# A feed-forward's first bias moved into its weights, relu and split in one ScalarE pass, the inverse root on GpSimd

## The chip, the core and the metric

The kernel runs on one core of a Trainium2 chip. The time is that of the device from the first to the last instruction of the program, in microseconds; the lower the better. Of three runs before the change the median is 1888.09 us (1886.04 to 1891.85). The profile is of one further execution.

The engines, as the profile names them: PE (TensorE's matrix multiplications) and PEld (its weight loads), DVE (VectorE), ACT (ScalarE), POOL (GpSimd), and SP (SyncE, which here only issues transfers). Each engine works through its own queue in order.

## What is computed

A macaron block on x of shape (8, 2048, 256), all in float32: half a feed-forward, a state space layer (SSM) with a skip and a layer norm, half a feed-forward.

```python
def _layernorm(x, axis=-1, eps=1e-05):
    m = jnp.mean(x, axis=axis, keepdims=True)
    v = jnp.var(x, axis=axis, keepdims=True)
    return (x - m) / jnp.sqrt(v + eps)

# feed-forward; w1 is (256, 1024), w2 is (1024, 256)
    h = jax.nn.relu(jnp.einsum('bsd,dw->bsw', x, w1) + b1)
    return jnp.einsum('bsw,wd->bsd', h, w2) + b2

# SSM: K is a kernel of 2048 lags per channel, from the parameters
    z = y + x * D[None, None, :]          # y = causal convolution of x with K
    r = x + z
    out = (r - mu) * jax.lax.rsqrt(var + LN_EPS) * ln_w + ln_b

# the block
    x = x + 0.5 * _L0_ffn_ref(_layernorm(x, axis=-1), ...)
    x = x + _L0_attn_ref(_layernorm(x, axis=-1), ...)
    x = x + 0.5 * _L0_ffn_ref(_layernorm(x, axis=-1), ...)
```

Both feed-forwards have the same weights. Their layer norm has no weights of its own, so the 256 normalised channels of a token sum to zero.

## The kernel before

**Tiling.** The 16384 tokens are worked in 64 groups of 256 (two tiles of 128 tokens, `NTB = 2`). A feed-forward goes through the groups one by one (`sublayer`, L807). Each group has 8 steps, one for each block of 128 hidden units. A step multiplies up (`up`, L782: 6 matmuls of 128x128 by 256 columns), applies relu, and three steps later (`LAG = 3`) multiplies that block down (`down`, L793: 6 matmuls). So a group has 96 matmuls of 256 columns.

**Float32 out of three products.** Every factor is split into a rounded high part (type float32r) and a low part. A product is high x low + low x high + high x high, hence three matmuls for each. Weights are split once (`load_weights`, L149), the group's input once a group (xh, xl), and each hidden block once a step (hh, hl). The hidden block's path is: PE writes `ph` in PSUM; ScalarE applies relu with the first bias in place (L857); ScalarE copies the high part to `hh` (L858); VectorE subtracts to get the low part `hl` (L859). Four PSUM banks hold `ph`.

**The group's input.** `ffn_in` (L709) takes the group's rows, makes mean and variance on VectorE (`stats`, L659), the half root on ScalarE (`root`, L670), a polished inverse root on VectorE (`rstds`, L676: four instructions on 128x2 numbers), and normalises (`norm`, L686). In groups 0 to 11 of the first feed-forward (`ACT_NORM = 12`) the normalisation runs on ScalarE, elsewhere on VectorE. GpSimd then adds half the second bias to the rows (L719). The normalised rows are turned by PE in groups 0 to 13 and 19 to 43 of the first feed-forward and 0 and 1 of the second (L726, then xh on ScalarE L735 and xl on VectorE L737). In the others they are turned by the DMA engines in two 16-bit halves (`turn_by_dma`, L742: halves apart on both engines L747, store, transposing load, halves together L765, xh L767, xl L769). The buffer `xn` of the normalised rows is single and is shared with `y` of the second feed-forward and with `sw` of the convolution.

**The order of work.** `pre_a` and `pre_b` (L893, L1118) make a group's input in steps, one for each step of the loop, and begin 18 and 19 steps ahead of the group's turn. `post_a` (L903) adds the group's output, stores x1, and normalises it into `u`, the SSM's input, with another root and polish; `post_b` (L1144) adds and stores. During the first feed-forward a background generator (`matrices`, L234, then `early`, L1050) makes the SSM's matrices from the parameters: first some 150 small steps on VectorE, then tables on GpSimd, then for 32 batches six products of 128x512 on GpSimd (`make`, L557, lines L570 to L580). Each batch is then split, stored, and transposed by DMA (L590, L620). The background is handed out by a budget: each loop step adds 1.32, and a batch of matrices takes 8.0 of it. Apart from that the order on each engine is that of a planner, which simulates the program and puts instructions in queues as they become ready; before the first group ScalarE and VectorE keep program order.

**The second feed-forward.** `pre_b` loads x1 through SP's queue into `xb`, has GpSimd add the layer norm's bias (L1125), makes statistics of the convolution's output on VectorE, root and polish, `y` (L1135) and then x2 (L1138), and goes through `ffn_in`. `xb` has five buffers.

Of the kernel before, what the change touches and what calls it, by code (L numbers as in the profile page):

```python
# [29 lines left out]
# pi / 2 in four parts, the first three of eight bits each  # L30
# [13 lines left out]
def macaron_s4d_kernel(  # L44
# [25 lines left out]
    NJ = L // P           # chunks of 128 positions  # L70
    CB = (NJ - 1) * B     # columns (chunk, batch) of the chunks that have a next one
    NQ = 4                # quarters of the sequence
# [3 lines left out]
    NTB = 2               # token tiles in a group  # L76
    TOK = NTB * P
    NG = NJ * B // NTB    # groups
    GPJ = B // NTB        # groups in a chunk
# [3 lines left out]
    NZ = 1  # L83
    PINF = 0
# [3 lines left out]
    NU = NFC // 2         # units of two blocks of the hidden layer  # L88
    SLOTS = 2 * NU        # steps in a group

    NPAIR = H // 2        # channels h = 2 g + c; (c, n) on the partitions
    NK = 8                # powers w**(2**k)
    NA, NB = 8, 16        # w**(16 a + b), below 128
    BCH = 8               # channels in a batch of matrices, in two parts
    NBT = H // BCH
    HCH = BCH // 2
    PB = BCH // 2         # pairs in a batch
    KROW = 256            # the lags from 128 to 0, then 127 zeros
# [9 lines left out]
    BUFS = {"e": 1, "te": 1, "x": 5, "xn": 1, "xh": 2, "xl": 2, "hh": 4, "hl": 4, "pl": 2, "g": 1, "gt": 1}  # L108
# [4 lines left out]
    def slot(tag, shape, name, dtype=F32):  # L113
        tag = {"sw": "xn"}.get(tag, tag)
        return work.tile(shape, dtype, name=name, tag=tag, bufs=BUFS[tag])

# [9 lines left out]
    # The SSM's input, then its output in place: [position in chunk, chunk, batch, channel].  # L126
    u = upool.tile([P, NJ, B, H], F32, name="u")
    # Until their quarters of the input come: room for the SSM's matrices.
# [4 lines left out]
    # ------------------------------------------------------------- weights  # L133
# [6 lines left out]
    b1_sb = const.tile([P, NFC], F32, name="b1_sb")  # L140
    hb2 = const.tile([P, H], F32, name="hb2")
    eps4 = const.tile([P, 1], F32, name="eps4")
    V.memset(eps4, 0.25 * EPS)
    A_.activation(stat.tile([P, 1], F32, name="warm", tag="s"), eps4, AF.Sqrt)
# [4 lines left out]
    def load_weights():  # L149
# [4 lines left out]
        raw2 = room[1][:, NDC * W : NDC * W + NFC * H].rearrange("p (f m) -> p f m", m=H)  # L154
        w2v = w2.rearrange("(fc p) m -> p fc m", p=P)
        for i in range(4):
# [3 lines left out]
            )  # L160
        for i in range(2):
            fs = slice(4 * i, 4 * i + 4)
            W2Q[i].dma_start(out=raw2[:, fs], in_=w2v[:, fs, :])
        for _ in range(7):
            yield
        for i in range(4):
            fs = slice(i * q, (i + 1) * q)
            hi = w1t[0][:, :, fs]
            A_.copy(hi, raw1[:, i])
# [18 lines left out]
    # ------------------------------------------------------- the SSM's matrices  # L188
    # P[n, k] = p0 w**k with p0**2 = 2 Ct w: a chunk's state is sum_k P[n, 127 - k] u[k], and
    # position i of the next chunk takes Re(sum_n P[n, i] state[n]).  # L190
# [4 lines left out]
    # w**128, and its imaginary part with the signs for the conjugate states  # L195
# [27 lines left out]
    def vsqrt(o, v, t, s, pace):  # L223
        """o = sqrt(v), to float32's precision."""
# [481 lines left out]
    def halves(xt):  # L706
        return [xt[:, i, :] for i in range(NTB)]
# [481 lines left out]
```

## Time and profile before

| | us |
|---|---|
| median of three runs | 1888.09 |
| the profiled execution, its span | 1885.0 |
| first matmul of the first feed-forward | 9.2 |
| first feed-forward, up to its last relu | 857.4 |
| second feed-forward, first to last relu | 1139.8 to 1877.5 |
| PE busy | 1813.4 (96%) |
| DVE busy | 1566.6 (83%) |
| ACT busy | 1267.4 (67%) |
| POOL busy | 726.0 (39%) |

How to read the rows. In the page's slices each digit is the busy share of one fortieth of the span in tenths. PEclk is the clock that TensorE was granted, in tenths of full speed. A row of groups reads: line, engine, operation, output<-inputs, shape, count | busy us, mean ns of one | idle time of the engine just before, and what ended it. A row of waits reads: who waited <- for whom: total us, times, longest us. A row of the chain or of the timeline: start us, length us, what. A busy PE is not PE at its full rate, since matmuls overlap; the distance from start to start tells that.

### The profile page before, as it was taken

To read this page: it belongs to the slowest core of one execution; us is meant where nothing else is said; L and a number is where in the kernel's file an instruction comes from. 1 tells how busy PE (TensorE), PEld (TensorE's weight loads), DVE (VectorE), ACT (ScalarE), POOL (GpSimd) and SP (SyncE) were. 2 spreads that over 40 slices of the span, in tenths; PEclk is the share of its full clock that TensorE was granted. 3 is DMA by queue.
4 is the path that set the end of the run, shared out by engine and by line. 5 is a ranking of instruction groups with operands and counts; after the bars stand their busy time and mean duration, and the time that the engine had idled before them with its cause. 6 is when DMAs were issued, how large, how long until landed. Compare 5 with 4: busy or idle time off the path is not lost.

```text
span 1885.0 us, 41022 instructions
## 1 busy us (share of the span) xinstructions
PE 1813.4 (96%) x14091; PEld 1797.2 (95%) x14091; DVE 1566.6 (83%) x5027; ACT 1267.4 (67%) x3027; POOL 726.0 (39%) x963
## 2 busy tenths in 40 slices
PE   7999899889989999999999988999999999999999
PEld 7998889889988999999999988999999999999998
DVE  5999897988899867757666648999888999999995
ACT  6776556767767767766566645767777776677775
POOL 1117753888488115111866621222222222222220
PEclk9999999999999999999999998999999999999999
DMA  5111224798879743345667681333333333333331
GB/s 188 45 45 50 80 80 129 215 251 243 242 224 254 207 107 94 92 118 162 174 179 198 183 246 51 91 90 94 94 94 90 92 95 90 92 94 91 93 93 52
DMA packets 329140, 245.31 MB, mean 130 GB/s; under 512 B 170467, under 2 KB 275683, under 8 KB 328419
## 3 DMA queue, kind: packets, MB, share of 16 engines
q1 hardware_dynamic: 327152, 241.76, 45.9%
q8 instruction: 111, 1.82, 0.4%
q0 software_dynamic: 800, 0.67, 0.2%
q14 instruction: 99, 0.80, 0.1%
q10 hardware_dynamic: 978, 0.26, 0.1%
HBM read 91.89 MB, written 111.15 MB: 108 GB/s over the span
## 4 chain that ended last, share of the span: by engine, by line
PE 65%; DVE 2%; DMA 1%; issue 0%; ACT 0%; DVEq 0%; ACTq 0%
PE po_b L798 19%; PE ph_b L788 19%; PE po_a L798 7%; PE ph_a L788 6%; PE py L1036 6%; PE pv L970 5%; PE py L1041 3%; DMA tz<-kpad 1%; PE pe L1072 0%; DVE hl_a L859 0%; DVE xb L118 0%; DVE st_r L663 0%; DVE u L620 0%; DVE y L118 0%; DVE u L696 0%
## 5 line engine op out<-in xcount | busy, mean ns | idle before, releaser
L788 PE MATMUL ph_a<-xh_a,wa 128*128 128x256 f32 x2048 | 460.2, 289 | 7.6 <-ACT xh_a L735 3.7
L788 PE MATMUL ph_b<-xh_b,wb 128*128 128x256 f32 x2048 | 442.4, 284 | 0.7 <-ACT xh_b L735 0.7
L798 PE MATMUL po_a<-wa,hh_a 128*128 128x256 f32 x2048 | 393.3, 285 | 0.0
L798 PE MATMUL po_b<-wb,hh_b 128*128 128x256 f32 x2048 | 387.5, 283 | 0.0
L788 PEld LDWEIGHTS ph_a<-xh_a,wa 128*128 128x128 f32 x2048 | 361.7, 196 | 9.2 <-ACT xh_a L735 5.6
L857 ACT ACTIVATE ph_a<-ph_a,b_sb 128x256 f32<-128x256 f32 x512 | 228.8, 449 | 189.5 <-PE ph_a L788 179.1
L788 PEld LDWEIGHTS ph_b<-xh_b,wb 128*128 128x128 f32 x2048 | 352.5, 193 | 1.1 <-ACT xh_b L735 1.1
L857 ACT ACTIVATE ph_b<-ph_b,b_sb 128x256 f32<-128x256 f32 x512 | 230.3, 451 | 162.2 <-PE ph_b L788 151.4
L798 PEld LDWEIGHTS po_a<-wa,hh_a 128*128 128x128 f32 x2048 | 323.2, 194 | 0.2 <-issue 0.2
L798 PEld LDWEIGHTS po_b<-wb,hh_b 128*128 128x128 f32 x2048 | 319.2, 192 | 0.0
L788 PE MATMUL ph_a<-xl_a,wa 128*128 128x256 f32 x1024 | 294.4, 290 | 20.7 <-DVE xl_a L769 11.2
L798 PE MATMUL po_a<-wa,hl_a 128*128 128x256 f32 x1024 | 299.6, 293 | 9.0 <-DVE hl_a L859 8.5
L1125 POOL TENSOR_TENSOR xb<-xb,lnb_sb 128x512 f32<-128x512 f32 x64 | 94.4, 1475 | 530.6 <-DMA xb<-x_dram 329.0
L798 PE MATMUL po_b<-wb,hl_b 128*128 128x256 f32 x1024 | 292.7, 286 | 0.3 <-DVE hl_b L859 0.2
L788 PE MATMUL ph_b<-xl_b,wb 128*128 128x256 f32 x1024 | 286.5, 284 | 0.1
L859 DVE TENSOR_TENSOR hl_a<-ph_a,hh_a 128x256 fp32r<-128x256 f32 x512 | 206.9, 411 | 82.6 <-ACT hh_a L858 80.9
L859 DVE TENSOR_TENSOR hl_b<-ph_b,hh_b 128x256 fp32r<-128x256 f32 x512 | 205.1, 410 | 37.6 <-ACT hh_b L858 36.0
L788 PEld LDWEIGHTS ph_a<-xl_a,wa 128*128 128x128 f32 x1024 | 201.3, 197 | 23.1 <-DVE xl_a L769 12.2
L719 POOL TENSOR_TENSOR xa<-xa,hb 128x512 f32<-128x512 f32 x64 | 84.3, 1317 | 350.6 <-DVE xn_a L696 239.3
L798 PEld LDWEIGHTS po_a<-wa,hl_a 128*128 128x128 f32 x1024 | 198.5, 194 | 14.4 <-DVE hl_a L859 14.0
L798 PEld LDWEIGHTS po_b<-wb,hl_b 128*128 128x128 f32 x1024 | 196.3, 192 | 1.6 <-DVE hl_b L859 0.8
L788 PEld LDWEIGHTS ph_b<-xl_b,wb 128*128 128x128 f32 x1024 | 197.2, 193 | 0.4 <-DVE xl_b L737 0.3
(281 smaller groups left out, 3589.7 us busy)
## 6 DMA issues: line engine op xcount, KB each, us to landing
xa<-in_L_attn_x_dram SPq DMA_DIRECT2D x64, 256.0 KB, 2.8
x_dram<-xa SPq DMA_DIRECT2D x64, 256.0 KB, 2.3
o<-u SPq DMA_DIRECT2D x64, 256.0 KB, 4.0
pv<-planes SPq DMA_DIRECT2D x32, 512.0 KB, 3.5
pt<-u SPq DMA_DIRECT2D x32, 512.0 KB, 3.6
ot<-o SPq DMA_DIRECT2D x64, 256.0 KB, 3.5
tz<-kpad SPq DMA_DIRECT2D x64, 256.0 KB, 3.8
xb<-x_dram SPq DMA_DIRECT2D x64, 256.0 KB, 2.8
```

The costliest lines, as they stand in the source:

```text
L719: G_.tensor_add(xt, xt, hb2.unsqueeze(1).to_broadcast([P, NTB, H]))
L788: nc.tensor.matmul(ph, wt[wp][:, dc, fs], xp[:, dc, :], start=(n == 0), stop=(n == 3 * NDC - 1))
L798: nc.tensor.matmul(po[:, i, :], hp[:, tsl], wt[wp][:, fc, :], start=(fc == 0 and i == 0 and n == 0), stop=(fc == NFC - 1 and n == 2), skip ...
L857: A_.activation(ph, ph, AF.Relu, bias=b1_sb[:, fc : fc + 1])
L859: last[V] = V.tensor_sub(hl, ph, hh.bitcast(F32))
L970: nc.tensor.matmul(pv[:, l, :], pt[:, l, :], u[:, 0 : NJ - 1, :, BCH * bt + 2 * l + c], start=True, stop=True,)
L1036: nc.tensor.matmul(py[:, l, :], u[:, :, :, BCH * bt + 2 * l + c].rearrange("p j b -> p (j b)"), tz[:, l, :], start=(l == 0), stop=False, s ...
L1041: nc.tensor.matmul(py[:, l, :], xs[:, c, p0 + l, :], ot[:, l, :], start=False, stop=(l == PB - 1), skip_group_check=True,)
L1125: G_.tensor_add(xt, xt, lnb_sb.unsqueeze(1).to_broadcast([P, NTB, H]))
```

## The change

- **First bias.** `w1`'s last row is subtracted from all its rows, and the bias is put in place of the last row (which has become zero). The last of the 256 normalised channels is set to one instead of its value. Since the channels sum to zero, the product is the same with the bias in it. The bias tile and its small load go; two loads on ScalarE's queue bring the last row and the bias to all 128 partitions.
- **Relu and split.** ScalarE's relu writes the high part `hh` straight from PSUM. VectorE's low part is max(ph, 0) - hh, from the raw product.
- **Inverse root.** ScalarE's root and VectorE's polish are gone. GpSimd adds eps and raises to -1/2 with a tensor of exponents.
- **Normalisation.** In both feed-forwards the group's input is normalised on ScalarE, in all groups, on 255 channels. The negated mean times the inverse root, its bias, is made on GpSimd in two instructions. For `u` the choice stays as it was (ScalarE up to group 11, VectorE after), with one loop step between root and use.
- **Buffers.** `xn` is a fixed single tile, whose last channel is set to one at the start and again after the convolution, which still uses it as `sw`. `y` gets two buffers of its own.

```diff
+    xns = [const.tile([P, NTB, H], F32, name=f"xn{i}") for i in range(NXN)]
+    for xn in xns:
+        G_.memset(xn[:, :, H - 1 : H], 1.0)
     hb2 = const.tile([P, H], F32, name="hb2")
-    eps4 = const.tile([P, 1], F32, name="eps4")
-    V.memset(eps4, 0.25 * EPS)
+    power = const.tile([P, NTB], F32, name="power")
+    V.memset(power, -0.5)
...
+        nc.scalar.dma_start(out=last, in_=w1[H - 1].partition_broadcast(P))
+        nc.scalar.dma_start(out=bias, in_=b1.partition_broadcast(P))
...
             hi = w1t[0][:, :, fs]
+            V.tensor_sub(
+                raw1[:, i], raw1[:, i], last[:, fs].unsqueeze(1).to_broadcast([P, NDC, q])
+            )
+            stt(raw1[:, i, NDC - 1], bias[:, fs], ident[:, P - 1 : P], raw1[:, i, NDC - 1], ALU.mult, ALU.add)
             A_.copy(hi, raw1[:, i])
             V.tensor_sub(w1t[1][:, :, fs], raw1[:, i], hi.bitcast(F32))
...
-    def root(mv, name):
-        s = stat.tile([P, NTB], F32, name=f"s_{name}", tag="s")
-        A_.activation(s, mv[:, :, 1], AF.Sqrt, bias=eps4, scale=0.25)
-        return s
...
-    def rstds(mv, s, name):
+    def rstds(mv, name):
         t = stat.tile([P, NTB], F32, name=f"t_{name}", tag="tt")
-        q = stat.tile([P, NTB], F32, name=f"q_{name}", tag="q")
-        V.reciprocal(t, s)
-        stt(q, mv[:, :, 1], EPS, t, ALU.add, ALU.mult)
-        stt(q, q, 0.25, s, ALU.mult, ALU.add)
-        V.reciprocal(t, q)
+        G_.tensor_scalar_add(t, mv[:, :, 1], EPS)
+        G_.tensor_tensor(t, t, power, op=ALU.pow)
         return t
 
     def norm(dsts, srcs, mv, rs, name, on_act=False):
         if on_act:
             nb = stat.tile([P, NTB], F32, name=f"nb_{name}", tag="nb")
-            stt(nb, mv[:, :, 0], -1.0, rs, ALU.mult, ALU.mult)
+            G_.tensor_mul(nb, mv[:, :, 0], rs)
+            G_.tensor_scalar_mul(nb, nb, -1.0)
...
-        s = root(mv, f"f{name}")
-        yield
-        rs = rstds(mv, s, f"f{name}")
-        yield
-        xn = slot("xn", [P, NTB, H], f"xn_{name}")
-        norm(halves(xn), halves(xt), mv, rs, f"f{name}", on_act)
+        rs = rstds(mv, f"f{name}")
+        yield
+        yield
+        xn = xns[turn_xn[0] % NXN]
+        turn_xn[0] += 1
+        norm(
+            [xn[:, i, 0 : H - 1] for i in range(NTB)], [xt[:, i, 0 : H - 1] for i in range(NTB)],
+            mv, rs, f"f{name}", on_act,
+        )
         G_.tensor_add(xt, xt, hb2.unsqueeze(1).to_broadcast([P, NTB, H]))
...
-                A_.activation(ph, ph, AF.Relu, bias=b1_sb[:, fc : fc + 1])
-                last[A_] = A_.copy(hh, ph)
-                last[V] = V.tensor_sub(hl, ph, hh.bitcast(F32))
+                last[A_] = A_.activation(hh, ph, AF.Relu)
+                last[V] = stt(hl, ph, 0.0, hh.bitcast(F32), ALU.max, ALU.subtract)
...
-        return (yield from ffn_in(xt, f"a{g}", g < ACT_NORM, by_dma))
+        return (yield from ffn_in(xt, f"a{g}", True, by_dma))
...
         mv = stats(halves(xt), f"u{g}")
         yield
-        s = root(mv, f"u{g}")
-        yield
-        rs = rstds(mv, s, f"u{g}")
+        rs = rstds(mv, f"u{g}")
+        yield
         norm(ucols(g), halves(xt), mv, rs, f"u{g}", g < ACT_NORM)
...
+    for xn in xns:
+        G_.memset(xn[:, :, H - 1 : H], 1.0)
+    ys = wpool.tile([P, 2, NTB, H], F32, name="ys", tag="wE")
...
-        rs = rstds(mv, s, f"r{g}")
-        yield
-        y = slot("xn", [P, NTB, H], f"y_{g}")
+        rs = rstds(mv, f"r{g}")
+        yield
+        yield
+        y = ys[:, g % 2]
...
-        return (yield from ffn_in(xt, f"b{g}", False, by_dma))
+        return (yield from ffn_in(xt, f"b{g}", True, by_dma))
```

More of the change, by code (lines that the diff above doesn't have):

```diff
@@ L83, in macaron_s4d_kernel @@
     NZ = 1
+    NXN = 1
     PINF = 0
@@ L107, in macaron_s4d_kernel @@
     BANKS = {"h": 4, "t": 1, "o": 2, "b": 1}
-    BUFS = {"e": 1, "te": 1, "x": 5, "xn": 1, "xh": 2, "xl": 2, "hh": 4, "hl": 4, "pl": 2, "g": 1, "gt": 1}
+    BUFS = {"e": 1, "te": 1, "x": 5, "xh": 2, "xl": 2, "hh": 4, "hl": 4, "pl": 2, "g": 1, "gt": 1}
     def bank(tag, name):
@@ L113, in slot @@
     def slot(tag, shape, name, dtype=F32):
-        tag = {"sw": "xn"}.get(tag, tag)
         return work.tile(shape, dtype, name=name, tag=tag, bufs=BUFS[tag])
@@ L138, in macaron_s4d_kernel @@
     w2_dram = dram.tile([2, P, NFC, H], F32, name="w2_dram")
-    b1_sb = const.tile([P, NFC], F32, name="b1_sb")
+    xns = [const.tile([P, NTB, H], F32, name=f"xn{i}") for i in range(NXN)]
+    for xn in xns:
+        G_.memset(xn[:, :, H - 1 : H], 1.0)
     hb2 = const.tile([P, H], F32, name="hb2")
-    eps4 = const.tile([P, 1], F32, name="eps4")
-    V.memset(eps4, 0.25 * EPS)
-    A_.activation(stat.tile([P, 1], F32, name="warm", tag="s"), eps4, AF.Sqrt)
+    power = const.tile([P, NTB], F32, name="power")
+    V.memset(power, -0.5)
+    warm = const.tile([P, 1], F32, name="warm")
+    V.memset(warm, 1.0)
+    A_.activation(warm, warm, AF.Sqrt)
     W1Q = [nc.sync] * 4
@@ L154, in load_weights @@
         raw2 = room[1][:, NDC * W : NDC * W + NFC * H].rearrange("p (f m) -> p f m", m=H)
+        last, bias = (
+            room[1][:, NDC * W + NFC * H + i * W : NDC * W + NFC * H + (i + 1) * W] for i in range(2)
+        )
         w2v = w2.rearrange("(fc p) m -> p fc m", p=P)
@@ L712, in ffn_in @@
         yield
-        s = root(mv, f"f{name}")
+        rs = rstds(mv, f"f{name}")
         yield
-        rs = rstds(mv, s, f"f{name}")
         yield
-        xn = slot("xn", [P, NTB, H], f"xn_{name}")
-        norm(halves(xn), halves(xt), mv, rs, f"f{name}", on_act)
+        xn = xns[turn_xn[0] % NXN]
[3 more added lines that the diff above has]
+            mv, rs, f"f{name}", on_act,
+        )
         G_.tensor_add(xt, xt, hb2.unsqueeze(1).to_broadcast([P, NTB, H]))
@@ L780, in macaron_s4d_kernel @@
     turned_ = [0]
+    turn_xn = [0]
     def up(wt, xT, ph, fc):
@@ L1017, in stack @@
         A_.copy(xs[0:N, 1, pairs], sw)
+    sw = xns[0].rearrange("p i h -> p (i h)")[0:N, 0 : PB * CB].rearrange("n (g m) -> n g m", g=PB)
     def outputs(gr):
@@ L1022, in outputs @@
             if c == 0:
-                stack(xs[:, :, :, B:], slice(p0, p0 + PB), slot("sw", [N, PB, CB], f"sw{bt}"))
+                stack(xs[:, :, :, B:], slice(p0, p0 + PB), sw)
             i = (2 * bt + c) % 3
@@ L1084, in macaron_s4d_kernel @@
     nc.gpsimd.dma_start(out=hb2, in_=b2.partition_broadcast(P))
-    with nc.allow_non_contiguous_dma(reason="1024 numbers, once"):
-        nc.gpsimd.dma_start(out=b1_sb, in_=b1.rearrange("(fc p) -> p fc", p=P))
     G_.tensor_scalar_mul(hb2, hb2, 0.5)
@@ L1128, in pre_b @@
         yield
-        s = root(mv, f"r{g}")
+        rs = rstds(mv, f"r{g}")
         yield
-        rs = rstds(mv, s, f"r{g}")
         yield
-        y = slot("xn", [P, NTB, H], f"y_{g}")
+        y = ys[:, g % 2]
         for i in range(NTB):
```

## The prediction, made before the changed kernel was run

> **What bounds the kernel now.** I first read the page's slices. PE's digits are 8 or 9 nearly everywhere, so what has to be found is where it is held up, and by whom.
>
> ```profile
> PE   7999899889989999999999988999999999999999
> DVE  5999897988899867757666648999888999999995
> POOL 1117753888488115111866621222222222222220
> PEclk9999999999999999999999998999999999999999
> ```
>
> A slice is 47 us. The first feed-forward ends near slice 18, the convolution near slice 24, the second feed-forward is the rest. VectorE is as full as PE wherever a feed-forward runs, and POOL is full only in slices 3 to 12, where the SSM's matrices are made.
>
> Then I cut the span into stages by the first relu of each group (64 groups of 8 relus per feed-forward): groups 0 to 11, 12 to 22, 23 to 46, 47 to 63, and the second feed-forward. Columns are length, busy time of PE, its weight loads, VectorE, ScalarE, POOL, then the granted clock.
>
> ```profile
> 13.00:163.00 150.00, 145.24 (x1182) 143.13 (x1182) 129.20 (x503) 105.45 (x276) 32.17 (x33) 0.99 0.21 70
> 163.00:319.00 156.00, 143.23 (x1153) 140.87 (x1152) 137.74 (x402) 90.68 (x227) 85.32 (x82) 0.98 0.29 81
> 319.00:651.00 332.00, 304.58 (x2394) 297.64 (x2393) 300.14 (x801) 238.94 (x527) 232.26 (x189) 0.96 0.88 238
> 1140.00:1870.00 730.00, 729.54 (x6053) 728.05 (x6052) 665.19 (x2123) 513.80 (x1323) 171.39 (x122) 1.00 0.33 89
> ```
>
> Per group that is 12.5, 14.2, 13.8 us in the three stretches of the first feed-forward. In the second, the chain of work that ended last consists of matmuls alone, and two groups take 23.13 us:
>
> ```profile
> 1186.46 1.92 PE ph_b L788 x16
> 1209.59 1.92 PE ph_b L788 x16
> ```
>
> Two groups are 192 matmuls, so 120.4 ns each: 11.56 us for a group, with no idle PE. So the second feed-forward can't become faster by this change, only slower. What can be won lies between 163 and 651. PE's waits there, for 319 to 651:
>
> ```profile
> PE ph_a L788 <- DVE xl_a L737: 9.1, 5, 2.4
> PE pt_a L726 <- DVE xn_a L696: 7.8, 5, 2.2
> PE po_a L798 <- DVE hl_a L859: 4.3, 9, 1.1
> PE ph_a L788 <- ACT xh_a L735: 3.7, 2, 3.1
> ```
>
> With one of 2.2 us more they sum to 27.1 us, nearly all for VectorE. The granted clock of 0.96 takes (1 - 0.96) x 332 = 13.3 us more; it dips to half for 3.4 to 6.8 us around these same gaps. So 332 - 40.4 = 291.6 us is PE's own need: 12.15 us a group. The same sum for 163 to 319: waits 12.7, clock 3.1, own need 140.2 (12.75 a group, with the kernel matmuls of L522). Both stretches are held up by a VectorE that is late.
>
> **The change, part by part.** *VectorE loses the root's polish and the feed-forward's normalisation.* In 319 to 651 these rows cost (columns: busy, mean ns):
>
> ```profile
> L118 DVE SCALAR_TENSOR_TENSOR q_fa<-q_fa,s_fa 128x2 f32<-128x2 f32 x25 | 11.9, 475 | 0.0
> L118 DVE SCALAR_TENSOR_TENSOR q_u<-q_u,s_u 128x2 f32<-128x2 f32 x24 | 11.5, 480 | 0.1
> L696 DVE TENSOR_SCALAR xn_a<-xa,mv_fa,t_fa 128x256 f32<-128x256 f32 x50 | 26.6, 572 | 0.2
> ```
>
> Two elements take 475 ns; in the second feed-forward the same step takes 162. The polish of a group is 475 + 281 + 159 + 157 for the feed-forward and 480 + 410 + 160 + 158 for u, 2.28 us; the normalisation 2 x 0.572. VectorE falls by 3.4 of its 300.1 / 24 = 12.5 us a group, to 9.1, under PE's 12.15. The split's lower part (L859, 0.41 us) becomes a scalar_tensor_tensor with constants; both forms stand side by side in the weights' preparation, 128x512, at 0.68 us each, so I count no change.
>
> *ScalarE.* The relu (L857, 450 ns) and the copy (L858, 374 ns) become one pass. If it costs the dearer 450, 8 x 0.374 = 3.0 us a group go; two roots of 0.29 go; two normalising passes of 0.598 (row L692) come. From 238.94 / 24 = 9.96 to 7.6 us. It is nowhere the bound, but it now waits for POOL before it normalises, and behind it in the queue stand the next relus, whose outputs VectorE and then PE need. The step loop uses a hidden block three steps (4.3 us) after it is begun; that covers a wait of some 3 us. Without that cover each us of waiting is a us of PE.
>
> *POOL gets six small instructions a group* in either feed-forward: add and power for each of the two normalisations, and two multiplies for the bias of the one on ScalarE (groups 0 to 11: eight). The nearest rows of the trace are the scan's 64-column products on POOL, from start to start 0.25 us:
>
> ```profile
> 942.24 0.29 POOL L1006 TENSOR_TENSOR gt<-xsA,wi_c 128x64 f32<-128x64 f32 x1
> 942.50 0.32 POOL L1007 TENSOR_TENSOR xsA<-xsA,g 128x64 f32<-128x64 f32 x1
> ```
>
> Two columns are less work and a dependent step adds about 0.1, so 0.2 each: four plain ones are 0.8 us. The power has no row. Its lower end is a plain step, 0.2 us. [...]
>
> In 319 to 651 POOL makes matrices: six instructions of 1118, 1286, 1391, 1137, 1151 and 1392 ns a batch, 7.48 us, a batch for every 8.0 / 1.32 = 6.06 steps of 8 in a group: 9.87 us a group. L719 adds 1.34, the new plain steps 0.8, two powers 0.8: **12.8 us against PE's 12.15.** POOL is in order, the normalisation now waits for it, so POOL sets the pace there: 24 x 12.8 = 307 us for 332, a gain of 25 (40 if POOL keeps up).
>
> [...]
>
> 163 to 319: POOL has 85.3 / 11 = 7.75 us a group, with 1.6 more far below 12.75. But single steps of the tables last 1 to 2 us and can make the power late. I take 10 of the 15.8 us.
>
> *Start.* The weights' preparation gains two broadcast loads on ScalarE's queue, 0.5 MB each, and two VectorE steps a quarter (0.68 and about 0.42) ahead of the split. From 5 to 20 us the DMA engines are full, at 303 to 410 GB/s; 1 MB takes about 3 us of that. First matmul at 9.2 us now: plus 3 and 1.1, so 4 us later, with ends of 1.1 (the loads hide) and 7. Small gain behind it: 4.5 us of waits for hl before 163, of which I take 1.5. The small bias load on POOL's queue goes; nothing waited for it.
>
> *Second feed-forward.* VectorE falls further below PE, and ScalarE too; POOL has 171.4 / 63 = 2.7 us a group and gets 1.6. y has its own two buffers in place of sharing one with the normalised input; nothing waited for that by name. 0 us.
>
> Sum: +4 - 1.5 - 10 - 25 = -32.5 on 1885.0, 1852.5. The runs' median, 1888.09, lies 3.1 above the profiled execution: **1856 us**.
>
> **Rivals.** *Full relief*: POOL keeps up, all 56.2 us of waits and clock dips go, 4 are lost at the start and 1.5 won: 1885.0 - 53.7 + 3.1 = 1834. Some 5 us of gaps will stay: 1839. For it: VectorE is named for nearly every wait. Against it: POOL's 12.8.
>
> *A slow power, which ends slower.* The stretch from 319 takes 24 x (12.0 + 2p) us. With the other terms the gain is used up at p = 1.1 us. At p = 2, 384 us, 52 lost, 5 won before it and 2.5 lost at the start: about 1938. [...]
>
> *The queue's order in the second feed-forward.* L1125 heads POOL's queue and waits for the transfer of xb, 310 us in total between 1140 and 1870. In one pair of groups it runs from 1418.4 to 1419.7, while the normalisation of a nearer group ran at 1414.8. If that group's add, power and multiplies (1.2 us) stood behind it, its input would be 6.1 us later. The transposed halves land at about 1422.1 and are taken at 1424.7, so 2.5 us are covered: 3.6 us in every second group, 115 us in all. In one pair of six it is 19 us, and 1856 becomes 1875; in one of three, the gain is gone. Against it: the statistics are ready at 1412.9, and the transfer is issued only at 1414.1.
>
> *Nothing*: lateness moves from VectorE to POOL one for one, 1885 to 1892.
>
> **How the numbers follow.** Chances: the sum 0.48, full relief 0.22, slow power 0.12, order 0.11 (mostly slower), nothing 0.07. Likeliest, 1856. The sum's own range, with the ends of start, power and the two stretches, is 1842 to 1878. To leave out 2 in 10 the range goes from 1834 (full relief) to 1910 (the mild part of the slow cases). Runs of this kernel differ by 0.3%, which is what can be told from no change. Faster by more 0.70, within 0.07, slower by more 0.23.
>
> **What would show it.** Right: between 319 and 651 the groups at 12.5 to 13 us, PE's waits for xl and xn small, POOL above 90% busy, the power's row at 0.3 to 0.6 us, VectorE near 9 us a group; the first matmul at 12 to 14 us; 23.1 us for two groups in the second feed-forward. Wrong: a power above 1 us; PE waiting in the second feed-forward for xh or hl behind an ScalarE normalisation; or POOL's matrix steps becoming so much shorter without VectorE's two-input steps that the groups reach 12.15.

## The result, and the profile after

The changed kernel takes **1978.78 us** (median of 4 runs, 1976.54 to 1994.77) against 1889.97 us for the kernel before in the same runs (4 runs, 1886.04 to 1892.46): a ratio of 1.0487, 95% interval 1.0447 to 1.0527. The forecast was 1856, with a range of 1834 to 1910. It was wrong in its sign. The profiled execution of the changed kernel spans 1974.8 us, that of the kernel before 1885.0, so 89.8 us have to be found.

Line numbers in this part are those of the changed kernel: relu L868, its lower part L118 (`stt`), addition of eps L688, power L689, the two multiplies for the bias of the normalisation L695 and L696, the normalisation on ScalarE L699, the half second bias L729. In the second feed-forward: load of a group's rows L1137, addition of ln_b L1138, last addition L1158, output store L1161. In the variants below the numbers shift by up to eight lines.

First the same slices of the page as before, and under them the page's chain of work by engine:

```profile
PE   6999799998998999999999889899999989999999
DVE  5897876767787666557676366666666656666665
POOL 3348865999897446217665444344434344443441
...
PE 43%; DMA 21%; DVE 16%; POOL 10%; ACT 5%; issue 4%; SPq 1%; ACTq 0%; POOLq 0%; DVEq 0%
```

VectorE's digits fell in both feed-forwards, from 8 and 9 to 6 and 7, as the change intends. POOL's rose from 2 to 4 in the second feed-forward (right half). PE is not visibly emptier: a loss of 10% of a stage hides in digits of 9. The chain tells it. The same row of the kernel before, whose chain reaches back over only 68% of the span, was

```profile
PE 65%; DVE 2%; DMA 1%; issue 0%; ACT 0%; DVEq 0%; ACTq 0%
```

Now PE is 43%, and DMA, VectorE and POOL share nearly half.

Then the stages, cut as in the prediction. Two windows of the changed kernel, groups 23 to 46 and the second feed-forward (length, busy PE, weight loads, VectorE, ScalarE, POOL, granted clock, DMA share, GB/s):

```profile
330.00:655.00 325.00, 299.90 (x2394) 294.64 (x2393) 239.80 (x555) 176.24 (x336) 285.27 (x336) 0.97 0.89 242
...
1148.00:1967.00 819.00, 757.41 (x6114) 746.66 (x6114) 508.88 (x1505) 350.11 (x824) 324.75 (x496) 0.99 0.30 80
```

In the last line PE is idle for 61.6 of 819 us; in the second feed-forward of the kernel before it was idle for 0.5 of 730. A granted clock of 0.99 in place of 1.00 takes some 8 us more (an estimate, 0.01 x 819). By the start of the first relu of the groups that bound them, the stages are, in us:

| stage | before | after | difference |
|---|---|---|---|
| to the first relu | 12.9 | 24.2 | +11.3 |
| groups 0 to 11 | 150.5 | 146.9 | -3.6 |
| groups 12 to 22 | 155.2 | 158.7 | +3.5 |
| groups 23 to 46 | 332.8 | 325.7 | -7.1 |
| groups 47 to 63 | 206.0 | 202.7 | -3.3 |
| convolution, to the first relu of the second feed-forward | 282.3 | 289.8 | +7.5 |
| second feed-forward, first to last relu | 737.8 | 819.3 | +81.5 |

Behind the last relu both need 7.4 to 7.5 us. So nine tenths of the loss arise in the stage to which the prediction gave 0 us, and the stage that was to bring 25 us brings 7. The waits in the second feed-forward, all engines:

```profile
POOL t_fb L688 <- DVE mv_fb L682: 263.4, 62, 5.8
DVE pl_b L757 <- ACT xn L699: 231.8, 62, 5.4
ACT xn L699 <- POOL nb_fb L696: 206.9, 59, 5.0
...
POOL xb L1138 <- DMA xb<-x_dram: 128.2, 59, 3.5
...
PE po_b L809 <- DVE hl_b L118: 61.5, 52, 2.5
```

Read from the bottom: PE waits for the lower part of the hidden block. VectorE makes that from ScalarE's relu, and ScalarE stands in front of its normalisation until POOL's bias is there, 59 times, 3.5 us each on average. POOL in turn stands in front of the addition of ln_b until the rows of another group have landed, again 59 times. One group in the timeline (start, duration, and in brackets the idle time before it with its releaser):

```profile
1503.17 0.36 POOL L688 TENSOR_SCALAR t_fb<-mv_fb 128x2 f32<-128x2 f32 x1 [4.20 <-DVE mv_fb L682]
1503.49 0.43 POOL L688 TENSOR_SCALAR t_r<-mv_r 128x2 f32<-128x2 f32 x1
1503.88 0.71 POOL L689 TENSOR_TENSOR t_fb<-t_fb,power 128x2 f32<-128x2 f32 x1
...
1504.55 0.69 POOL L689 TENSOR_TENSOR t_r<-t_r,power 128x2 f32<-128x2 f32 x1
...
1505.20 0.20 POOL L695 TENSOR_TENSOR nb_fb<-mv_fb,t_fb 128x2 f32<-128x2 f32 x1
1508.16 1.29 POOL L1138 TENSOR_TENSOR xb<-xb,lnb_sb 128x512 f32<-128x512 f32 x1 [2.75 <-DMA xb<-x_dram]
1509.53 0.24 POOL L696 TENSOR_SCALAR nb_fb<-nb_fb 128x2 f32<-128x2 f32 x1
1509.80 1.09 ACT L699 ACTIVATE xn<-xb,nb_fb,t_fb 128x255 f32<-128x255 f32 x2 [4.26 <-POOL nb_fb L696]
...
1511.45 1.20 ACT L868 ACTIVATE hh_b<-ph_b 128x256 fp32r<-128x256 f32 x4
```

The power is done at 1504.59 and the first multiply at 1505.40. The second multiply, 0.24 us of work that turns the sign, follows 4.1 us later, because the planner has put another group's addition (L1138) between the two in POOL's queue. In ScalarE's queue the relus of the group that PE works on stand behind the normalisation: four of them are let go together at 1511.45.

Why the addition is late, the chain of work tells for the same group (start, duration, what):

```profile
1500.23 0.60 DVE xb L1158
...
1501.41 2.89 DMA out_dram<-xb
...
1504.32 3.71 DMA xb<-x_dram
...
1508.16 1.30 POOL xb L1138
...
1509.53 0.25 POOL nb_fb L696
...
1509.80 1.10 ACT xn L699 x2
...
1511.45 0.38 ACT hh_b L868
...
1511.86 0.31 DVE hl_b L118
...
1513.74 0.60 DVE xb L1158
```

It is a closed loop. A group's last addition lets its output be stored (2.89 us). The buffer that the store frees takes the next rows (3.71 us). POOL adds ln_b to these, and only then finishes the bias of the nearer group. ScalarE normalises, the relus follow, and with them the last addition of the next group. Once round takes 13.51 us here, where PE needs 11.56 a group. Over the whole stage a group takes 819.3 / 64 = 12.8 us, 1.27 more than before.

### The profile page after: what moved, and what is told of

It reads as the page before. It is cut to its first block, busy times and chain, and to the rows that moved or that the text cites. A ratio compares the mean times of both kernels' runs of the same rounds, so it can differ in the third digit from the quotient of the medians.

```text
span 1974.8 us, 39019 instructions
## 1 busy us (share of the span) xinstructions
PE 1827.4 (93%) x14091; PEld 1804.8 (91%) x14091; DVE 1303.9 (66%) x3756; ACT 923.8 (47%) x1979; POOL 1038.5 (53%) x1756
## 4 chain that ended last, share of the span: by engine, by line
PE 43%; DMA 21%; DVE 16%; POOL 10%; ACT 5%; issue 4%; SPq 1%; ACTq 0%; POOLq 0%; DVEq 0%
PE po_a L809 12%; PE ph_a L799 12%; DMA out_dram<-xb 8%; DMA xb<-x_dram 8%; PE py L1047 5%; PE pv L979 5%; POOL xb L1138 4%; ACT xn L699 3%; DVE hl_b L118 3%; PE ph_b L799 3%; PE po_b L809 3%; PE py L1052 3%; DVE xb L118 2%; DVE xb L1158 2%; ACT hh_b L868 1%
## 5 line engine op out<-in xcount | busy, mean ns | idle before, releaser
L799 PEld LDWEIGHTS ph_a<-xh_a,wa 128*128 128x128 f32 x2048 | 358.8, 196 | 14.1 <-ACT xh_a L777 10.3
L809 PE MATMUL po_b<-wb,hl_b 128*128 128x256 f32 x1024 | 297.7, 291 | 61.6 <-DVE hl_b L118 61.5
L868 ACT ACTIVATE hh_a<-ph_a 128x256 fp32r<-128x256 f32 x512 | 191.7, 381 | 337.7 <-PE ph_a L799 287.4
L118 DVE SCALAR_TENSOR_TENSOR hl_a<-ph_a,hh_a 128x256 fp32r<-128x256 f32 x512 | 207.9, 414 | 161.8 <-ACT hh_a L868 159.7
L868 ACT ACTIVATE hh_b<-ph_b 128x256 fp32r<-128x256 f32 x512 | 176.4, 381 | 195.0 <-PE ph_b L799 191.7
L118 DVE SCALAR_TENSOR_TENSOR hl_b<-ph_b,hh_b 128x256 fp32r<-128x256 f32 x512 | 207.9, 416 | 59.4 <-ACT hh_b L868 58.3
L757 DVE COPY pl_b<-xn 128x512 uint16<-128x512 uint16 x62 | 26.5, 427 | 231.8 <-ACT xn L699 231.8
L699 ACT ACTIVATE xn<-xb,nb_fb,t_fb 128x255 f32<-128x255 f32 x128 | 69.9, 594 | 217.6 <-POOL nb_fb L696 217.6
```

Source lines behind the costliest of these rows:

```text
L118: return V.scalar_tensor_tensor(out=o, in0=a, scalar=s, in1=b, op0=op0, op1=op1)
L699: A_.activation(dst, src, AF.Identity, bias=nb[:, i : i + 1], scale=rs[:, i : i + 1])
L757: copy(pl[:, w], xu[:, :, :, :, w])
L799: nc.tensor.matmul(ph, wt[wp][:, dc, fs], xp[:, dc, :], start=(n == 0), stop=(n == 3 * NDC - 1))
L809: nc.tensor.matmul(po[:, i, :], hp[:, tsl], wt[wp][:, fc, :], start=(fc == 0 and i == 0 and n == 0), stop=(fc == NFC - 1 and n == 2), skip ...
L868: last[A_] = A_.activation(hh, ph, AF.Relu)
```

## The experiments

The stages of all runs, in us; the first number is a single run's time except in the lines marked with the number of runs. "Before" was measured on the same chip in each case and lies between 1886.44 and 1890.08.

| kernel | time | first relu | 0-11 | 12-22 | 23-46 | 47-63 | convolution | second feed-forward |
|---|---|---|---|---|---|---|---|---|
| e1_nb_dve | 1879.27 | 23.3 | 147.1 | 150.8 | 323.4 | 203.4 | 286.6 | 735.4 |
| e2_order | 1891.59 | 24.3 | 147.4 | 158.8 | 326.2 | 202.4 | 288.6 | 734.6 |
| e3_x7 | 1990.28 | 24.2 | 146.0 | 160.5 | 333.3 | 202.4 | 291.4 | 823.1 |
| e4_fold_only | 1895.07 | 20.9 | 145.5 | 155.6 | 328.3 | 204.0 | 290.2 | 741.3 |
| e5_roots_back | 1961.94 | 21.9 | 148.0 | 155.2 | 319.9 | 204.8 | 290.5 | 812.3 |
| e6_loads | 1884.45 | 22.4 | 146.7 | 155.9 | 324.7 | 203.2 | 286.8 | 735.5 |
| e7_start | 1884.52 | 22.5 | 146.7 | 155.8 | 323.0 | 203.3 | 288.6 | 735.4 |
| e8_share | 1874.50 | 23.2 | 146.2 | 146.8 | 321.6 | 203.2 | 288.7 | 735.5 |
| e9_twice | 1910.89 | 25.1 | 145.5 | 161.5 | 326.9 | 213.7 | 293.6 | 735.4 |
| e10_norm_act | 1898.80 | 21.0 | 147.9 | 152.2 | 333.2 | 204.0 | 291.7 | 739.6 |
| e11_fold_pool | 1878.88 | 24.6 | 148.4 | 148.6 | 320.6 | 203.2 | 288.6 | 735.6 |
| e12_share_timed (6 runs) | 1873.84 | 23.2 | 146.3 | 146.9 | 320.0 | 203.2 | 286.7 | 734.2 |
| e13_share_start (6 runs) | 1877.42 | 22.3 | 147.1 | 149.9 | 321.7 | 203.2 | 289.2 | 736.6 |

How far a single execution can be trusted: e8 and e12 are the same kernel, and lie within 2.0 us of each other in every stage. e3 and the changed kernel stand in the same order on every engine until the second feed-forward begins, and yet groups 23 to 46 took 333.3 us in the one and 325.7 in the other (granted clock 0.95 against 0.97 in the same 325 us). A difference of up to 8 us in that stage is therefore not read as an effect below.

**The loop in the second feed-forward.** The first experiment takes the two multiplies off POOL: the bias is one VectorE step again, as in the kernel before. Everything else of the change stays.

```
-            G_.tensor_mul(nb, mv[:, :, 0], rs)
-            G_.tensor_scalar_mul(nb, nb, -1.0)
+            stt(nb, mv[:, :, 0], -1.0, rs, ALU.mult, ALU.mult)
```

> The changed kernel, with the bias of the normalisation made by one VectorE instruction again, in place of two multiplies on POOL. The powers stay on POOL. Theory (queue order: the second multiply stands behind the add of the layer norm's bias, which waits for the transfer of xb, and so closes a loop from one group's output to a nearer group's input): nothing of a group's normalisation is behind that add any more, the second feed-forward takes 738 to 745 us from first to last relu in place of 819, and the whole about 1892. Rival A (the powers of 0.7 us and POOL's load set the pace): the two multiplies are only 0.4 us of 5 us a group, so the second feed-forward stays above 800. Rival B (normalising on ScalarE ahead of the relus is the cause): also above 800.

The second feed-forward fell to 735.4 us. The window of that kernel over 727 us of it:

```profile
1143.00:1870.00 727.00, 726.35 (x6051) 725.95 (x6050) 545.00 (x1541) 353.39 (x815) 290.89 (x365) 1.00 0.33 90
```

PE is idle for 0.65 us. POOL's own wait for the rows is still there (it is idle for 80.6 us ahead of the addition, L1137 here), but the bias of the nearer group no longer stands behind it.

That alone doesn't tell the order from the number of small POOL steps. The second experiment leaves all six steps on POOL and changes only where the addition stands: it keeps the place that the program gives it.

```
-        G_.tensor_add(xt, xt, lnb_sb.unsqueeze(1).to_broadcast([P, NTB, H]))
+        tc.keep_in_program_order(
+            G_.tensor_add(xt, xt, lnb_sb.unsqueeze(1).to_broadcast([P, NTB, H]))
+        )
```

> The changed kernel, with only the place of one POOL instruction pinned: the add of the layer norm's bias to xb keeps its program order, which puts it behind the multiplies of the group before it. No instruction more or less. Theory (queue order): second feed-forward 738 to 750 us, the whole about 1895. Rival A (powers and POOL's load) and rival B (ScalarE's normalisation) both: no change, about 819 and 1975.

734.6 us, with powers and multiplies on POOL. Its timeline of POOL:

```profile
1501.34 0.20 POOL L695 TENSOR_TENSOR nb_fb<-mv_fb,t_fb 128x2 f32<-128x2 f32 x1
1501.62 0.24 POOL L696 TENSOR_SCALAR nb_fb<-nb_fb 128x2 f32<-128x2 f32 x1
1503.64 1.53 POOL L729 TENSOR_TENSOR xb<-xb,hb 128x512 f32<-128x512 f32 x1 [1.77 <-ACT xn L699]
1505.12 1.29 POOL L1139 TENSOR_TENSOR xb<-xb,lnb_sb 128x512 f32<-128x512 f32 x1
```

The multiplies now follow one another within 0.28 us, the addition (L1139 here) comes last, and its rows have landed by then. The whole change stands in this kernel, and it takes 1891.59 us against 1890.08 before. On PE, VectorE and ScalarE the order differs from that of the changed kernel in 48, 36 and 8 places only, of 14091, 3756 and 1979. So the place of one instruction in POOL's queue accounts for 819.3 - 734.6 = 84.7 us.

The third puts the root back on ScalarE and VectorE, as before the change, and leaves the multiplies on POOL:

```
-        G_.tensor_scalar_add(t, mv[:, :, 1], EPS)
-        G_.tensor_tensor(t, t, power, op=ALU.pow)
+        A_.activation(s, mv[:, :, 1], AF.Sqrt, bias=eps4, scale=0.25)
...
+        q = stat.tile([P, NTB], F32, name=f"q_{name}", tag="q")
+        V.reciprocal(t, s)
+        stt(q, mv[:, :, 1], EPS, t, ALU.add, ALU.mult)
+        stt(q, q, 0.25, s, ALU.mult, ALU.add)
+        V.reciprocal(t, q)
```

> The changed kernel, with the roots on ScalarE and their polish on VectorE as before; the two multiplies stay on POOL, and stand there behind the add that waits for xb. Theory (queue order): the loop stays, the second feed-forward stays above 790 us. Rival A (the powers' 0.7 us): without powers it falls to about 740. Rival B (ScalarE's normalisation): stays near 819. First feed-forward, groups 23 to 46: POOL loses 3 of its 13.7 us a group; if POOL set the pace there, these groups fall from 325 us to below 310, unless VectorE's polish of 2.3 us a group takes that back.

The second feed-forward stayed at 812.3 us without a single power on POOL. The power's price, on which the rival of the slow power hung, has next to no part in the loss (812.3 us without powers, 819.3 with them, 735.4 in e1 with them). The place of the addition is a different one here (L1145, ahead of the multiplies L700 and L701):

```profile
1525.09 1.29 POOL L1145 TENSOR_TENSOR xb<-xb,lnb_sb 128x512 f32<-128x512 f32 x1 [8.12 <-DMA xb<-x_dram]
1526.34 0.20 POOL L700 TENSOR_TENSOR nb_fb<-mv_fb,t_fb 128x2 f32<-128x2 f32 x1
1526.62 0.22 POOL L701 TENSOR_SCALAR nb_fb<-nb_fb 128x2 f32<-128x2 f32 x1
```

It stands ahead of both multiplies. The loss therefore doesn't hang on the sign change alone: it comes with both multiplies behind the addition too. e10 below differs from this kernel only in making the bias on VectorE, and its second feed-forward takes 739.6 us. The loop is not the same step for step: between 1500 and 1530 the chain of this kernel also holds the transposing load of pt_b (14.7%).

The fourth asks whether the ring of five buffers is what makes the rows late. Two more are taken from the room of `ys`:

```
-    ys = wpool.tile([P, 2, NTB, H], F32, name="ys", tag="wE")
+    ys = wpool.tile([P, 4, NTB, H], F32, name="ys", tag="wE")
...
-        xt = xts[g] = slot("x", [P, NTB, H], f"xb_{g}")
+        xt = xts[g] = ys[:, g % 7 - 3] if g % 7 > 4 else slot("x", [P, NTB, H], f"xb_{g}")
```

> The changed kernel with seven buffers in place of five for the second feed-forward's rows, nothing else: the addition of ln_b still stands between the two multiplies of the bias in POOL's queue. Theory "the order in POOL's queue closes the loop, and the ring of five buffers is what makes the addition late": with two more buffers the rows land some 23 us earlier, the addition no longer waits, and the second feed-forward falls from 819 to 735 to 740 us, whole run about 1892 to 1898. Rival "the planner puts the loads just as late whatever the ring is, or the addition follows its group two further ahead and is again the last thing to land": 790 to 820 us, whole run 1950 to 1980.

823.1 us: my theory fell, and the rival held. The chain of work of this kernel:

```profile
1499.92 0.60 DVE xb L1158
...
1502.37 2.86 DMA out_dram<-xb
1505.25 2.87 DMA xb<-x_dram
...
1508.25 1.30 POOL xb L1138
...
1509.63 0.25 POOL nb_fb L696
```

The planner uses the new buffers to fetch rows further ahead, not to fetch the same rows earlier: the addition between the two multiplies of a group is for a group two further ahead than in the changed kernel. The load still goes out the moment a store has freed a buffer, and the addition behind it still stands between the two multiplies. So two more buffers don't open the loop; whether more would was not tried.

**What single parts are worth.** The next keeps the folded bias and the one-pass relu, and puts back root, bias of the normalisation and (from group 12 on) the normalisation on VectorE. Besides the edits of the first and third experiment:

```
-        return (yield from ffn_in(xt, f"a{g}", True, by_dma))
+        return (yield from ffn_in(xt, f"a{g}", g < ACT_NORM, by_dma))
...
-        return (yield from ffn_in(xt, f"b{g}", True, by_dma))
+        return (yield from ffn_in(xt, f"b{g}", False, by_dma))
```

> One part alone: the folded bias and the relu in one pass, with roots, polish and normalisation on the engines they had before. Theory: second feed-forward as before, 738 us (order on POOL as before); the start is later by about 9 us (loads and preparation, without the power's share), the first feed-forward's groups 12 to 46 a little faster than before, since ScalarE has 3 us a group less to do, but still held up by VectorE: 1885 to 1895 in all. Rival B predicts the same. Rival C (the single relu pass or the new form of the lower part costs in the second feed-forward): above 760 there.

1895.07 us. Fold and one-pass relu, with the new buffers of `xn` and `y` that every variant keeps, cost 8.0 us ahead of the first relu (20.9 against 12.9) and 7.9 in the convolution's stage. They bring 5.0 in groups 0 to 11. The second feed-forward is 3.5 longer. In groups 23 to 46 they take VectorE nothing off, and 328.3 against 332.8 is within the margin.

Folded bias with the normalisation on ScalarE, but without the powers, is the next: the edits of the first and third experiment together.

> Folded bias, one-pass relu and the feed-forward's normalisation on ScalarE stay as in the change; the inverse root is put back on ScalarE and VectorE and the bias of the normalisation is one VectorE step, so that nothing small is left on POOL. Theory "the root waits in POOL's queue behind 1.2 us matrix steps, ScalarE stands with its normalisation waiting for it, and the relus stand behind that": groups 23 to 46 at 314 to 320 us against 323.4 with the powers on POOL, groups 12 to 22 at 146 to 151, second feed-forward 735, whole run 1862 to 1872. Rival "VectorE's load decides, and the polish of the root is what fills it": 327 to 333 in groups 23 to 46, 155 in groups 12 to 22, whole run 1884 to 1892.

The rival's forecast for groups 23 to 46 came (333.2), and the time was even above its 1892. PE's waits in 320 to 650 of this kernel:

```profile
PE ph_a L804 <- DVE xl_a L752: 17.0, 12, 3.5
PE po_a L814 <- DVE hl_a L118: 9.9, 15, 1.4
```

With the polish back on VectorE the lateness is again mainly that of the split input, as in the kernel before. The powers on POOL are therefore worth having: e1 differs from this kernel in them alone and is 19.5 us faster, a single run each. By stages they bring 9.8 us in groups 23 to 46, 4.2 in the second feed-forward and 5.1 in the convolution, and cost 2.3 at the start. One thing contradicts a simple story of VectorE's load: e5 has the same roots and only the multiplies on POOL, and took 319.9 in groups 23 to 46. With an uncertainty of 8 us I leave the size of this term open.

**Is POOL the pace in groups 23 to 46?** The prediction said so: 12.8 us a group. Two experiments start from e1 and load POOL less and more. The first moves one of the six steps of each batch of matrices, the addition, to VectorE:

```
-            E.tensor_add(pi, pi, tm)
+            V.tensor_add(pi, pi, tm)
```

> As e1_nb_dve, with one of the six matrix products of a batch on VectorE in place of POOL (1.3 us of POOL for some 0.7 us of VectorE, 32 times; per group 1.8 and 0.9). Theory (POOL sets the pace of groups 23 to 46, 323 us in e1_nb_dve): these groups fall to about 300 us. Rival (VectorE or the DMA queues still set it): they stay at 320 or rise.

The second makes every power twice, the first time into a tile that nobody reads:

```
+        t0 = stat.tile([P, NTB], F32, name=f"t0_{name}", tag="t0")
+        G_.tensor_tensor(t0, t, power, op=ALU.pow)
         G_.tensor_tensor(t, t, power, op=ALU.pow)
```

> As e1_nb_dve, with each power computed twice (the first result is not used). Theory (POOL sets the pace of groups 23 to 46): 2 x 0.8 us a group more, 38 us more there, about 360; groups 12 to 22 a few us more; the second feed-forward, where POOL is idle for more than half the time, stays within 745 us. Rival for the second feed-forward (the power's latency is on its path): it rises by 20 us or more.

In groups 23 to 46 the lighter POOL gave 321.6 and the heavier 326.9, against 323.4. The added powers of the second are 18.8 + 17.9 = 36.7 us of work on POOL there, and the stage is 3.5 us longer. Eight matrix steps (9.8 us) slid into groups 47 to 63, so POOL is busy for 290 of 325 us, against 275 in e1 and 252 in e8. If POOL set the pace, the stage would have grown by nearly all of the 36.7 us, or 26.9 less the eight steps, so POOL does not set it. What the doubling does cost lies mostly elsewhere: 10.7 us in groups 12 to 22, 10.3 in groups 47 to 63, which took over the eight steps, 7.0 in the convolution's stage. The second feed-forward, with 0.7 us more for each power, is unmoved (735.4). And in groups 12 to 22, where the prediction saw POOL far from full, taking an addition off it won 4.0 us. Other starts alone move that stage by as much (150.8 in e1, 155.8 and 155.9 in e7 and e6), so the 4.0 is weak evidence.

What is left is what stands ahead of the small steps. A gap of 2.99 us on PE in e8, which ends at 604.06, in the timeline:

```profile
597.85 1.52 POOL L585 TENSOR_TENSOR u<-u 128x512 f32<-128x512 f32 x1 [1.65 <-DMA pt<-u]
599.35 1.05 POOL L591 TENSOR_TENSOR u<-u 128x512 f32<-128x512 f32 x1
600.36 0.70 POOL L689 TENSOR_TENSOR t_fa<-t_fa,power 128x2 f32<-128x2 f32 x1
...
601.10 1.01 DVE L118 SCALAR_TENSOR_TENSOR nb_fa<-mv_fa,t_fa 128x2 f32<-128x2 f32 x1 [2.64 <-POOL t_fa L689]
...
602.19 1.09 ACT L698 ACTIVATE xn<-xa,nb_fa,t_fa 128x255 f32<-128x255 f32 x2 [5.19 <-issue]
603.18 0.36 ACT L867 ACTIVATE hh_a<-ph_a 128x256 fp32r<-128x256 f32 x1
...
604.06 0.38 PE L808 MATMUL po_a<-wa,hl_a 128*128 128x256 f32 x1 [2.99 <-DVE hl_a L118]
```

POOL is idle for 1.65 us in front of a matrix step whose input is in flight. The power stands behind that step and the next one, VectorE waits for the power, ScalarE's normalisation for VectorE, and the relu that PE needs is last in the row. It is the loop of the second feed-forward in small, and here it closes now and then instead of every time. Other gaps of this stage stand behind a copy that waits for its planes (in the changed kernel at 628.75 on VectorE, after 3.12 us of idling). How the 19 us of waiting for hl divide between these, no run here separates. A rival stands untested: the DMA engines are busy for 0.89 of this stage (0.88 before, 0.90 in e8), and the inputs that POOL and the copies wait for come through them. In e9 their share of 325 us fell to 0.78 and the stage was no shorter, which speaks against them, but no run changes their load alone.

**The start.** Two experiments on top of e1 move the new loads. In the first the weights' last row goes onto SP's queue ahead of the weights, and the bias to 32 partitions only:

```
-        nc.scalar.dma_start(out=last, in_=w1[H - 1].partition_broadcast(P))
-        nc.scalar.dma_start(out=bias, in_=b1.partition_broadcast(P))
...
+        nc.sync.dma_start(out=last, in_=w1[H - 1].partition_broadcast(P))
+        nc.sync.dma_start(out=bias[96:P], in_=b1.partition_broadcast(P - 96))
```

> As e1_nb_dve, with the two new broadcast loads behind the first group's rows on SP's queue in place of ScalarE's, and the bias for the 32 partitions that need it alone (0.13 MB for 0.5). Theory of the start (the loads share the DMA engines with the first group's rows, which land at 6.2 us for 3.7, and all that follows is late): the rows land near 3.7 us, the first relu comes near 20 us in place of 23.3, and the rest is as in e1_nb_dve: 1874 us. Rival (the preparation's longer chain on VectorE and ScalarE alone makes the start late): first relu stays above 22.5.

In the second the load of hb is issued earlier as well, and its halving on POOL is set behind the first powers:

```
-    G_.tensor_scalar_mul(hb2, hb2, 0.5)
...
+            if j == 5:
+                tc.keep_in_program_order(G_.tensor_scalar_mul(hb2, hb2, 0.5))
```

> As e6_loads, with the halving of the second bias on POOL behind the first group's power. In e1_nb_dve it stands ahead of it and waits for its load. Theory of the start: another 2 us, first relu at 17 to 19 us. Rival: no change against e6_loads, since the weights' own chain ends last.

Both win 0.8 to 0.9 us of 10.4. In e7 the first statistics are read at 3.62 us again, as in the kernel before, and it does not help: PE's waits until the first relu are for the first input, its upper and its lower part.

```profile
PE ph_a L804 <- ACT xh_a L750: 6.8, 1, 6.8
PE pt_a L741 <- ACT xn L704: 6.6, 1, 6.6
PE ph_a L804 <- DVE xl_a L752: 4.1, 1, 4.1
```

VectorE's timeline of the same kernel shows what stands ahead of the lower part:

```profile
8.96 1.66 DVE L183 TENSOR_TENSOR u<-u 128x512 f32<-128x512 f32 x1 [3.04 <-DMA u<-in_L_ffn_w_dram]
10.65 0.48 DVE L118 SCALAR_TENSOR_TENSOR u<-u,ident 32x256 f32<-32x256 f32 x1
...
19.41 0.68 DVE L752 TENSOR_TENSOR xl_a<-pt_a,xh_a 128x512 fp32r<-128x512 f32 x1
```

From 8.96 on, VectorE prepares three quarters of the first weights and parts of the second, 15 rows of 0.2 to 1.7 us with two other groups' statistics among them, before it comes to xl. In the kernel before only three such instructions stood ahead of it, and it ran at 10.18. The last of these experiments, on top of e8, gives the subtraction to POOL:

```
-            V.tensor_sub(
+            G_.tensor_sub(
                 raw1[:, i], raw1[:, i], last[:, fs].unsqueeze(1).to_broadcast([P, NDC, q])
```

> Bias of the normalisation as one VectorE step, the last addition of the matrices on VectorE, and the subtraction of the weights' last row (four steps, once, at the start) on POOL. Theory "VectorE's queue of the weights' preparation sets the start": POOL takes four steps of 1.3 us off VectorE, first relu at 19 to 21 us against 23.2, whole run about 1870 to 1872. Rival "the chain from the last row's landing through the first quarter's subtraction sets it": POOL's step is 0.6 us longer in that chain, first relu at 23.5 to 25, whole run 1874 to 1877. All other stretches as with the same kernel without this edit.

24.6 us against 23.2, as the rival had it: four instructions fewer on VectorE did not make the start earlier. That POOL's step is 0.6 us longer in the chain is an estimate (1.29 us for a 128x512 step on POOL, L1138 in the changed kernel, against 0.68 on VectorE); how long it took in this run was not shown.

**The best version found.** e8 in rounds, and e8 with the start of e7:

> The same kernel as e8_share, timed in rounds: bias of the normalisation as one VectorE step and the last addition of the matrices on VectorE. Theory "the gain between the groups 12 and 46 is a property of the schedule and not of one run": 1873 to 1876 us, ratio to the kernel before 0.991 to 0.993. Rival "one lucky run": 1878 to 1884.

> As e12_share_timed, with the two new loads moved from ScalarE's queue to SP's ahead of the weights (the bias to 32 partitions in place of 128), and the small load of hb and its halving on POOL set behind the first powers. Theory "the start's loads and the rest are independent terms": first relu at 22.4 against 23.2, all else alike, 1872 to 1875. Rival "another start makes another order of the steps, whose effect of up to 5 us in the groups 12 to 46 is larger than the term": 1876 to 1884.

e12 takes **1873.84 us** (1869.56 to 1875.82), a ratio of 0.9921 to the kernel before, interval 0.9907 to 0.9935. e13 takes 1877.42, ratio 0.9938 (0.9924 to 0.9952). e13's start is 0.9 us earlier, and 3.0 us are lost again in groups 12 to 22, so the rival's view of it (another start makes another order) fits better. The stages in the table are of one execution each, the fastest of e12's six and the slowest of e13's. The changed kernel with two small edits, the bias on VectorE and one addition of the matrices on VectorE, is thus 0.8% faster than the kernel before, where the change as it stands is 4.9% slower.

## Why the prediction was wrong, by its own steps

**Second feed-forward, "0 us": this step failed.** It compared totals: VectorE and ScalarE get less to do, POOL has room. All three were true (POOL is busy for 325 of 819 us), and 81.5 us were lost. The rival "the queue's order in the second feed-forward" named the instruction, the queue and the wait, and its price of 1.8 us a group (115 us in all) is of the order of the 1.27 measured (81.5). It got a chance of 0.11 because of one argument: "the statistics are ready at 1412.9, and the transfer is issued only at 1414.1". That argument took the add, the power and the multiplies for one block of 1.2 us that starts when the statistics are ready. They are six instructions, each with a place of its own in the queue, and the last of them, the one that the normalisation needs, was placed behind the addition. In the changed kernel at 1503 the statistics are still ready before the transfer is issued (1503.17 against 1504.32), and this saves nothing. The rival had two things wrong. It put all four steps behind the addition, where it was the last alone, the sign change. And it let the lateness come in every second group or less often; ScalarE waited for the bias 59 times in 64 groups.

**Groups 23 to 46, "-25": the mechanism was wrong.** -7.1 in a single execution, inside the margin of 8 us; 320 to 327 us in most variants with powers on POOL. "POOL sets the pace there" rested on 12.8 us a group against PE's 12.15. That sum took 9.87 us of matrices from the budget, where the prediction's own window had all of POOL's work of the stretch, L719 with it, at 232.26 / 24 = 9.7. With the new 1.6 us this is 11.3, less than PE's 12.15, so its own profile spoke against the step. Measured were 285.27 / 24 = 11.9; the powers were dearer than taken. The 0.4 us for each of them in "two powers 0.8" is shown by no run; in this stage they took 0.841 and 0.775. POOL was busy for only 88% of the stage while PE still waited, and the added powers of e9 moved the stage by 3.5 us for 36.7. VectorE fell from 12.5 to 10.0 us a group (forecast 9.1), ScalarE from 10.0 to 7.3 (forecast 7.6). Both are far below PE's 12.15, and the groups take 13.6. "Both stretches are held up by a VectorE that is late" is what the waits said; the step from there to VectorE's load read lateness as a lack of time. The new chain from POOL over ScalarE to VectorE brought the waits back under another name, with VectorE idle for a quarter of the stage: PE's waits for xl, xh and xn fell from 22.8 to 4.3 us, those for hl rose from 4.3 to 18.9, and the sum is 25.1 for 27.1.

```profile
PE po_a L809 <- DVE hl_a L118: 18.9, 14, 3.7
```

**Groups 12 to 22, "-10": wrong in sign** (+3.5). "1.6 more far below 12.75" is again a sum. What remains of a gain depends on what else stands in POOL's queue: with the bias on VectorE the stage took 150.8 us in e1 and 155.8 in e7, with one matrix step fewer on POOL 146.8 to 149.9. Groups 0 to 11 brought 3.6 us (1.5 taken), groups 47 to 63 another 3.3 that the sum didn't hold.

**Start, "+4, ends 1.1 to 7": mis-sized,** +11.3. The two extra steps were counted once, for the quarter that the first matmul needs. The first input's lower part stands in VectorE's queue behind three quarters, and it was the input, not the weights, that PE waited for. The first matmul came at 16.4 us (12 to 14 expected), the first relu another 7.8 later. Moving the loads, which got 3 of the 4 us, won 0.9. Fold and one-pass relu without the powers already cost 8.0, as e4 shows.

**Convolution's stage: not in the sum,** +7.5. About 2 us are PE's longer wait for the first normalised input of the second feed-forward (11.9 us, 9.9 before). Variants with and without powers have the rest too (286.6 to 291.7), so it comes with something that all of them keep, the fold, the one-pass relu or the new buffers of `xn` and `y`, and no run here says with which.

**Small prices.** The one-pass relu takes 381 ns, less than the two passes of before together (450 + 374 ns; taken: 450), and the lower part is unchanged (414 for 411). The four plain POOL steps take 0.37, 0.35, 0.29 and 0.24 us between 330 and 655 (taken: 0.2 each), 1.25 us a group in place of 0.8. In the second feed-forward, without matrix steps on POOL, the four take 0.20, 0.24, 0.43 and 0.36, 1.23 us, so together they cost the same in both stages. Of the three signs named for "wrong", "PE waiting in the second feed-forward for xh or hl" is what the profile shows. The powers took 0.69 to 0.84 us on average, not above 1, and POOL's matrix steps hardly became shorter: a batch's six took 7.22 us between 330 and 655, against 7.48 before, and no run shows that VectorE's two-input steps had anything to do with it.

## What to carry to other kernels

When a step moves to another engine, write down that engine's queue, instruction by instruction, with the waits of what is already in it. Here a step of 0.24 us behind a waiting one came 4.1 us late on an engine that was busy for 325 of 819 us, and four relus queued behind its consumer paid as well. If the last link of such a chain lets the transfer go out that the first waits for, it closes into a loop, and two more buffers did not open this one: look whether the chain of work repeats with DMA in it. To learn whether an engine's load sets the pace of a stage, double a small step on it, and see whether the stage grows by what was added.

## What the runs showed of the hardware that was not expected

In the changed kernel the power of two columns took 0.69 to 0.73 us on POOL where it made no matrices (second feed-forward) and 0.78 to 0.84 between matrix steps, in the second feed-forward some 3.5 times a plain multiply's 0.20. A plain addition of eps took 0.36 and 0.43 us there, more than the multiplies of the same size (0.20 and 0.24). A two-element VectorE step, the bias of the normalisation, which took 0.16 us in the second feed-forward of e1, took 1.01 us at 601.10 in e8, beside a matrix step on POOL (1.05 us from 601.04). And one order of instructions, run on two occasions, gave 325.7 and 333.3 us for the same 24 groups, with the granted clock at 0.97 and 0.95: stage times of single executions need a margin of that size.
